# Conditional residual layer: two copies of W1 go to GpSimd, more seeds, more W1 by id, and a key for every step

## The chip, the core and the metric

The kernel runs on one core of one Trainium2 chip. The core has five engines that each work through their own list of instructions in order: TensorE (PE in the profile, with its weight loads as PEld), VectorE (DVE), ScalarE (ACT), GpSimd (POOL) and SyncE (SP), which here issues nearly all DMAs. They wait for each other through semaphores. The metric is the device time of one launch in microseconds; smaller is better.

## The reference

There are 128 batches. Each has x of 128 rows and 512 columns (float32), and an id between 0 and 8 that picks one of ten sets of weights.

```python
w1 = W1[id]; w2 = W2[id]                       # 512x128, 128x512
h = relu(x @ w1 + b1[id])
y = x + h @ w2 + b2[id]
mean, var = moments of y over the 512 columns
out = x + (y - mean) * rsqrt(var + 1e-5) * gamma[id] + beta[id]
```

All of it is float32. x and out are 33.5 MB each.

## The kernel before

All ten sets of weights end up on chip as tables: W1 (`w1`), W2 (`w2`), and b2, gamma and beta spread over the 128 partitions (`b2_b`, `gamma_b`, `beta_b`). A batch then goes through these steps, in a software pipeline of several batches; the line numbers are those of the profile.

- SyncE loads x for four batches at a time, 1 MB, into one of four buffers (`load_x`, L83).
- TensorE turns x into x transposed, four matmuls against the identity (`transpose_x`, L330), and ScalarE copies it out of PSUM (`copy_xT`, L334).
- W1 of the batch's id is brought into a small tile `w1s`, of which there are seven buffers. In most batches ScalarE copies it from the table (`stage_w1`, L321). The first 17 batches load it from memory by id (L173).
- TensorE multiplies, "down" (L353, four matmuls into the one tile `ph`), ScalarE adds b1 and takes the relu (`relu`, L361), TensorE multiplies again, "up" (L375, or L367 in a seeded batch), into one of five tiles `ys` in PSUM.
- y = x + up + b2 needs one addition of x and one of b2. In a batch of kind P, GpSimd adds x and b2 into a tile r ahead of time (`add_b2`, L340; four buffers), and VectorE adds r to the result and sums its columns in one pass (`residual`, L393). In a batch of kind E, the "seeded" ones, ScalarE copies x into the PSUM tile before the up, which then adds onto it (`seed`, L316), and the residual adds the row of `b2_b`. A few early batches have b2 added by VectorE (L385), the first two and the last two by a matmul.
- ScalarE squares and sums (`square`, L416), takes the mean (L407) and the root (L426); VectorE refines the root in three short steps (L430, L432, L435), scales by gamma (`scale`, L459) and adds onto x + beta (`finish`, L468). GpSimd has put x + beta into the output tile before (`add_beta`, L347).
- SyncE stores a pair of batches, 512 KB, from one of eight pair tiles `os` (`store`, L472).

Letters for the turn of a batch: in an "F" batch, two in 16, x comes in by DMA a second time in blocks (L290) and VectorE finishes the transpose (`turn_blocks`, L302), so that TensorE has no transposes and ScalarE no copy; its W1 comes by id in matching rows (L296). In a "w" batch, one in 16, W1 is loaded by id (`load_late`, L582). All others are "T".

The order in which each engine gets its steps is a plan. Every step has a key, which is a batch number plus an offset; all steps are sorted by key and issued in that order, and each engine's own list is kept in it (`keep`). Offsets stand in small tables, one for the middle (`BATCH`, `PAIR`) and one for the edges (`BATCH_EDGE`, `EDGE`), so that every batch of a region has the same offsets:

```python
BATCH = dict(turn=0.19, copy=0.16, r=-0.36, beta=-0.13, relu=1.26, w1=-0.77, up=2.66, load=-5.59, r_late=0.22)
SEED = {'E': 1.69}
```

A store's key is just behind the key of its pair's second finish. The work ahead of batch 4 and the last eight or so batches (from E = 123 on, and parts of the five before) are written out by hand, outside the plan.

Of the kernel before, what the change touches and what calls it, by code (L numbers as in the profile page):

```python
# [13 lines left out]
ET = mybir.EngineType  # L14
# [3 lines left out]
G = 4  # L18
# [1 line left out]
FIRST = 17  # L20
EARLY = 17
LATE = 17
U = 2
MIDDLE = 26
TURNED = 32
LAST = 4
KINDS = 'EPPPPPEPEPPPEPPP'
TURNS = 'TTTTFTTTTwTTFTTT'
SEEDED = 'E'
ON_GPSIMD = 'P'  # L30
BATCH = dict(turn=0.19, copy=0.16, r=-0.36, beta=-0.13, relu=1.26, w1=-0.77, up=2.66, load=-5.59, r_late=0.22)
BATCH_EDGE = dict(copy=0.2, r=0.05, r_late=1.05, beta=1.06, relu=1.3, w1=-0.6, up=2.5)
SEED = {'E': 1.69}
PAIR = dict(stat=0.22, square=0.34, means=1.98, root=1.9, scale0=3.03, n1=2.43, n2=3.115, n3=3.28, scale1=3.4, end0=3.67, end1=4.32)
EDGE = dict(stat=0.6, square=0.68, means=1.75, root=1.77, scale0=2.64, n1=2.65, n2=3.592, n3=3.62, scale1=3.64, end0=3.66, end1=4.66)


@with_exitstack
def cond_resid_kernel(ctx: ExitStack, tc: tile.TileContext, x, itok, W1, b1, W2, b2, gamma, beta, out):
# [39 lines left out]
    E = B - 5  # L79
# [6 lines left out]
    def xb(b):  # L86
        return xs[b // G][:, b % G, :]
# [5 lines left out]
    w1 = const.tile([P, L, KC, A], FP, name="w1")  # L93
# [34 lines left out]
    parts = const.tile([P, H], BF, name="parts")  # L128
# [14 lines left out]
    lids, w1s = {}, {}  # L143
# [8 lines left out]
    def lid(b, engine):  # L152
        g = b // G
        if (g, engine) not in lids:
            loads, vals = nc.values_load_multi_w_load_instructions(
                lang[0:1, g * G : (g + 1) * G],
                engines=[engine],
                min_val=0,
                max_val=L - 1,
                skip_runtime_bounds_check_because="clamped on the chip to 0..L-1 above",  # L160
            )
            for ins in loads:
                keep(ins)
            lids[g, engine] = vals
        return lids[g, engine][b % G]
# [95 lines left out]
    xT, hT, rs, os, ys, ssqs, nmeans, rstds = {}, {}, {}, {}, {}, {}, {}, {}  # L261
    phs, pxs, sums = {}, {}, {}


    def b2_by_matmul(b):
        return b in (0, 1) or b >= B - 2

    def kind(b):
        return KINDS[b % len(KINDS)] if MIDDLE <= b < B - LAST else "-"

    def turn(b):
        return TURNS[b % len(TURNS)] if TURNED <= b < B - LAST - 2 else "-"

    def seeded(b):
        return kind(b) in SEEDED

    def b2_on_gpsimd(b):
        return kind(b) in ON_GPSIMD or kind(b) == "-" and not b2_by_matmul(b) and not b2_by_vector(b)

    def b2_by_vector(b):  # L280
        return kind(b) == "-" and (b in (2, 3, 9, 13, 17, 21) or 24 <= b < B - 8 and (b % 16 in (1, 6, 11) or b % 32 == 30))

    x2s = {}

# [32 lines left out]

    def stage_w1(b):
        w1s[b] = wp.tile([P, KC, A], FP, tag="w1s", name=f"w1s_{b}")
        src = w1.rearrange("p l k a -> p (l k a)")[:, bass.ds(lid(b, ET.Activation) * (KC * A), KC * A)]  # L320
        keep(nc.scalar.copy(w1s[b].rearrange("p k a -> p (k a)"), src))  # L321

    def transpose_x(b):
        pxs[b] = p_x.tile([P, KC, P], FP, tag="xT", name=f"pxT_{b}")
# [11 lines left out]
    def add_b2(b):  # L336
        if b2_on_gpsimd(b):
            rs[b] = rp.tile([P, H], FP, tag="r", name=f"r_{b}")
            v = lid(b, ET.Pool)
            keep(nc.gpsimd.tensor_tensor(rs[b], xb(b), b2_b[:, bass.ds(v * H, H)], ALU.add))  # L340

    def add_beta(b):
        g, j = divmod(b, 2)
        if j == 0:
            os[g] = op.tile([P, 2, H], FP, tag="o", name=f"o_{g}")
        v = lid(b, ET.Pool)
        keep(nc.gpsimd.tensor_tensor(os[g][:, j, :], xb(b), beta_b[:, bass.ds(v * H, H)], ALU.add))  # L347
# [61 lines left out]
    def square(b):  # L409

        g, j = divmod(b, 2)
        if j == 0:
# [61 lines left out]
    def on(b):  # L474
        return 0 <= b < B
# [172 lines left out]
    def at(when, step, *args):  # L648
        plan.append((when, len(plan), step, args))

    for b in range(B):
        when = BATCH_EDGE if kind(b) == "-" else BATCH
        if b >= 20 and b % G == 0:
            at((11 if b == 20 else b - 7) - 0.01, load_x, b // G)
        if b >= 3:
            for n, engine in ((b + 5, ET.Activation), (b + 5, ET.PE), (b + 6, ET.Pool)):
                if on(n):
                    at(b + 0.99, lid, n, engine)
        if turn(b) in "Fw":
            at(b + BATCH["load"] - 1, lid, b, ET.SP)  # L660
            at(b + BATCH["load"], load_rows if turn(b) == "F" else load_late, b)
        if turn(b) == "F":
            at(b + BATCH["load"], load_blocks, b)
            at(b + BATCH["turn"], turn_blocks, b)
        elif 5 <= b <= E - 2:
            at(b, transpose_x, b)
            at(b + when["copy"], copy_xT, b)
        if 4 <= b <= E - 3:
            at(b + (when["r"] if seeded(b) else when["r_late"]), add_b2, b)
            at(b + when["beta"], add_beta, b)  # L670
            at(b + 1.1, down, b)
            at(b + when["relu"], relu, b)
        if seeded(b):
            at(b + SEED[kind(b)], seed, b)
        if FIRST <= b <= E - 1 and turn(b) not in "Fw":
            at(b + when["w1"], stage_w1, b)
        if 2 <= b <= E - 4:
            at(b + when["up"], up, b)
# [4 lines left out]
    def at_pair(g, when, step, *args):  # L683
        if g < E // 2 - 3 or (step, *args) in begun:
            at(2 * g + 3 + when, step, *args)

    for g in range(E // 2 - 1):
        b = 2 * g
        when = EDGE if "-" in (kind(b), kind(b + 2)) else PAIR
        for j in (0, 1):  # L690
            at_pair(g, j + when["stat"] - 0.01, vector_b2, b + j)
            at_pair(g, j + when["stat"], residual, b + j)
            at_pair(g, j + when["square"], square, b + j)
        at_pair(g, when["means"], scalar_means, g)
        at_pair(g, when["root"], deviation, g)
        if b % G == 0 and on(b + G):
            at_pair(g, when["end0"] + 0.001, lid, b + G, ET.DVE)
        for n in (1, 2, 3):
            at_pair(g, when[f"n{n}"], rstd, g, n)
        for j in (0, 1):  # L700
            at_pair(g, when[f"scale{j}"], scale, b + j)
            at_pair(g, when[f"end{j}"], finish, b + j)
# [14 lines left out]
    copy_xT(E - 1)  # L717
    residual(E - 4)
    square(E - 4)
    rstd(E // 2 - 3, 3)  # L720
    relu(E - 2)
# [5 lines left out]
    end_of(E - 7)  # L727
    residual(E - 3)
    stage_w1(E)
    beta_of(E - 1)  # L730
    scalar_means(E // 2 - 2)
# [164 lines left out]
```

## Time and profile before

| what | value |
|---|---|
| median of three runs | 301.42 us (300.80 and 1073.14 the others) |
| profiled execution | 301.23 us, span 298.8 us |
| granted TensorE clock | 0.997 |
| busy: PE, DVE | 97%, 97% |
| busy: ACT, POOL | 93%, 93% |
| DMA | 85.48 MB, mean 286 GB/s, queue of SP 85.1% of 16 engines |

The span runs from the first to the last instruction; the profiled execution's own time has 2.4 us around it. Times of parts are read from the span. Busy shares are averages over the start (tables are loaded and spread, up to some 20 us), the long middle and the end (some 20 us), so the middle is looked at by itself. "L353" is line 353 of the kernel before.

### The profile page before, as it was taken

How to read it: one execution, taken by the hardware profiler on the slowest of the kernel's cores; microseconds unless marked ns; L12 is line 12 of the kernel's file. 1: busy time of each engine (PE TensorE's matmuls, PEld its weight loads, DVE VectorE, ACT ScalarE, POOL GpSimd, SP SyncE). 2: the span in 40 equal slices, each digit the busy share in tenths (PEclk: the TensorE clock that was granted, in tenths of full speed). 3: DMA queues.
4: the chain of work that ended last, by engine and by line, in shares of the span. 5: the costliest groups of instructions: out<-in, count | busy, mean ns of one | idle time of the engine just before them, and what ended most of it. 6: DMA issues, size and time to landing. Idle time of an engine off the chain costs nothing.

```text
span 298.8 us, 7251 instructions
## 1 busy us (share of the span) xinstructions
PE 290.7 (97%) x1783; PEld 214.7 (72%) x1783; DVE 288.9 (97%) x775; ACT 277.2 (93%) x766; POOL 277.4 (93%) x233
## 2 busy tenths in 40 slices
PE   7899999999999999999999999999999999999993
PEld 3758777777777777777777777777777777777761
DVE  6989999999999999999999999999999999999995
ACT  5868789999999999999999999999999999999983
POOL 1299998999999999999999999999999999999962
PEclk9999999999999999999999999999999999999998
DMA  6999999996799697988888887898988698894715
GB/s 233 369 393 370 342 329 396 400 325 212 270 297 328 169 378 218 321 316 284 277 280 295 275 283 256 281 300 224 356 256 269 233 313 301 250 349 163 237 73 219
DMA packets 61195, 85.48 MB, mean 286 GB/s; under 512 B 3641, under 2 KB 25156, under 8 KB 61154
## 3 DMA queue, kind: packets, MB, share of 16 engines
q1 hardware_dynamic: 61094, 84.97, 85.1%
q8 instruction: 15, 0.25, 0.3%
q14 instruction: 26, 0.21, 0.2%
q10 hardware_dynamic: 60, 0.05, 0.1%
HBM read 51.45 MB, written 33.55 MB: 284 GB/s over the span
## 4 chain that ended last, share of the span: by engine, by line
PE 81%; DVE 6%; ACT 4%; DMA 3%; issue 3%; SPq 1%; DVEq 0%; POOL 0%; ACTq 0%; POOLq 0%
PE ph L353 33%; PE py L375 26%; PE pxT L330 15%; PE py L367 7%; DMA w<-in_L_cond_W_dram 3%; DVE py L393 2%; ACT sq L416 1%; DVE o L553 1%; DVE py L459 1%; ACT w1s L321 1%; ACT xT L334 1%; SPq L173 1%; DVE n L559 0%; ACT hT L361 0%; ACT root L426 0%
## 5 line engine op out<-in xcount | busy, mean ns | idle before, releaser
L347 POOL TENSOR_TENSOR o<-x,beta_b 128x512 f32<-128x512 f32 x121 | 155.8, 1306 | 12.9 <-DVE beta_b L259 11.6
L353 PE MATMUL ph<-xT,w1s 128*128 128x128 f32 x1024 | 136.4, 276 | 0.1
L353 PEld LDWEIGHTS ph<-xT,w1s 128*128 128x128 f32 x1024 | 125.0, 192 | 8.7 <-ACT hT L361 7.0
L340 POOL TENSOR_TENSOR r<-x,b_b 128x512 f32<-128x512 f32 x89 | 116.1, 1305 | 0.0
L375 PE MATMUL py<-w,hT 128*128 x208 | 106.7, 595 | 0.7 <-DMA w<-in_L_cond_W_dram 0.7
L330 PEld LDWEIGHTS pxT<-ident,x 128*128 128x128 f32 x468 | 60.4, 150 | 60.6 <-issue 41.6
L459 DVE SCALAR_TENSOR_TENSOR py<-py,nmean,gamma_b 128x512 f32<-128x512 f32 x124 | 93.3, 753 | 0.0
L468 DVE SCALAR_TENSOR_TENSOR o<-py,rstd,o 128x512 f32<-128x512 f32 x116 | 86.8, 748 | 0.0
L416 ACT ACTIVATE sq<-py,sum 128x512 f32<-128x512 f32 x124 | 85.6, 690 | 0.7 <-DVE rstd L435 0.2
L334 ACT COPY xT<-pxT 128x512 f32<-128x512 f32 x117 | 67.8, 580 | 6.0 <-PE pxT L330 5.8
L330 PE MATMUL pxT<-ident,x 128*128 128x128 f32 x468 | 71.2, 275 | 0.9 <-ACT gamma_b L244 0.7
L393 DVE SCALAR_TENSOR_TENSOR py<-py,r 128x512 f32<-128x512 f32 x94 | 64.9, 690 | 1.4
L321 ACT COPY w1s<-w 128x512 f32 x91 | 56.7, 623 | 0.0
L361 ACT ACTIVATE hT<-ph,b1T 128x128 f32<-128x128 f32 x128 | 47.6, 372 | 5.1 <-PE ph L353 3.4
L375 PEld LDWEIGHTS py<-w,hT 128*128 128x128 f32 x208 | 31.7, 192 | 2.1 <-DMA w<-in_L_cond_W_dram 1.2
L416 ACT ACTIVATION_READ_ACCUMULATOR sq<-py,sum 128x1 f32 x124 | 25.9, 209 | 0.0
L367 PE MATMUL py<-w,hT 128*128 x48 | 25.3, 610 | 0.0
L393 DVE SCALAR_TENSOR_TENSOR py<-py,b_b 128x512 f32<-128x512 f32 x24 | 16.6, 693 | 1.5 <-PE py L367 1.4
L426 ACT ACTIVATE root<-ssq,eps 128x2 f32<-128x2 f32 x62 | 16.5, 266 | 1.5
L316 ACT COPY py<-x 128x512 f32<-128x512 f32 x24 | 14.4, 599 | 0.0
L393 DVE DVE_READ_ACCUMULATOR py<-py,r 128x1 f32 x94 | 13.2, 140 | 0.0
L407 ACT ACTIVATE nmean<-sum 128x2 f32<-128x2 f32 x61 | 11.7, 192 | 0.0
(79 smaller groups left out, 139.8 us busy)
## 6 DMA issues: line engine op xcount, KB each, us to landing
out_dram<-o SPq DMA_DIRECT2D x62, 512.0 KB, 4.0
x<-in_x_dram SPq DMA_DIRECT2D x27, 1024.0 KB, 7.7
w1s<-in_L_cond_W_dram SPq DMA_DIRECT2D x26, 256.0 KB, 7.3
x<-in_x_dram SPq DMA_DIRECT2D x10, 512.0 KB, 6.0
w1s<-in_L_cond_W_dram SPq DMA_DIRECT2D x44, 64.0 KB, 3.2
x<-in_x_dram SPq DMA_DIRECT2D x44, 64.0 KB, 2.1
w<-in_L_cond_W_dram SPq DMA_DIRECT2D x4, 640.0 KB, 8.1
w<-in_L_cond_W_dram SPq DMA_DIRECT2D x1, 1792.0 KB, 10.2
```

The lines of the kernel that those rows point to most:

```text
L321: keep(nc.scalar.copy(w1s[b].rearrange("p k a -> p (k a)"), src))
L330: keep(nc.tensor.transpose(pxs[b][:, k, :], cols, ident))
L334: keep(nc.scalar.copy(xT[b], pxs.pop(b)))
L340: keep(nc.gpsimd.tensor_tensor(rs[b], xb(b), b2_b[:, bass.ds(v * H, H)], ALU.add))
L347: keep(nc.gpsimd.tensor_tensor(os[g][:, j, :], xb(b), beta_b[:, bass.ds(v * H, H)], ALU.add))
L353: nc.tensor.matmul(phs[b], lhsT=w1s[b][:, k, :], rhs=xT_of(b, k), start=(k == 0), stop=(k == KC - 1))
L361: keep(nc.scalar.activation(hT[b], phs.pop(b), AF.Relu, bias=b1T[:, bass.ds(lid(b, ET.Activation), 1)]))
L375: keep(nc.tensor.matmul(ys[b], lhsT=hT[b], rhs=w2[:, bass.ds(v * H, H)], start=not m, stop=True))
L393: nc.vector.scalar_tensor_tensor(ys[b], ys[b], 1.0, r, ALU.mult, ALU.add, accum_out=sum_of(b))
L416: nc.scalar.activation(sq, ys[b], AF.Square, bias=col(sums, b), scale=-float(H), accum_out=col(ssqs, b))
L459: nc.vector.scalar_tensor_tensor(ys[b], ys[b], col(nmeans, b), gamma_b[:, bass.ds(v * H, H)], ALU.add, ALU.mult)
L468: nc.vector.scalar_tensor_tensor(o, ys[b], rstds[g][:, j : j + 1], o, ALU.mult, ALU.add)
```

## The change

Kinds and turns are now given in three strings: for the first 32 batches, for 16 that repeat from batch 32 to 111, and for the last 16.

- In the repeating part, seeded batches go from 4 in 16 (positions 0, 6, 8, 12) to 6 (0, 2, 6, 10, 12, 14). The other batches there have b2 added by GpSimd, as before. In the last 16 batches one is seeded (three before).
- "w" (W1 loaded by id) is at positions 0, 1, 2 (before: 9); in the last 16 at six batches (before one). "F" stays at 4 and 12, and at batch 116.
- A new turn, "c": `stage_w1` of such a batch is a `tensor_copy` on GpSimd in place of the copy on ScalarE, from the same table. Positions 8 and 14, and batch 121.
- Every step of every batch has its own offset, from a table `STEPS`: 32 values, then 16 that repeat, then 16. The loads of x have theirs in `X_STEPS`. Stores have keys of their own, too.
- An output tile or a tile of square sums is taken by whichever batch of the pair comes first.

```diff
-KINDS = 'EPPPPPEPEPPPEPPP'
-TURNS = 'TTTTFTTTTwTTFTTT'
+KINDS = ('MMDDPPPPPDPPPDPPPDPPPDPPPPPPEPPP', 'EPEPPPEPPPEPEPEP', 'PPEPPPPPPPPPPPMM')
+TURNS = ('TTTTTTTTTTTTTTTTTTTTTTTTTTTTTTTT', 'wwwTFTTTcTTTFTcT', 'TwTwFwwwwcTTTTTT')
...
+STEPS = {
+    "load": (
...
+        (-2.78, -1.96, -3.28, 0, -4.24, 0, 0, 0, 0, 0, 0, 0, -6.24, 0, 0, 0,),
...
+    "w1": (
...
+        (0, 0, 0, -0.79, 0, -0.39, 0.09, 0.85, -6.2, -3.35, -0.9, 0.28, 0, -0.7, -0.27, 0.84,),
...
+    "r": (
...
+        (0, -0.77, 0, -0.57, -0.65, -1.15, 0, 0.4, -0.76, 2.76, 0, -0.94, 0, 1.5, 0, -0.07,),
...
+    "beta": (
...
+        (3.06, 2.96, 3.37, 0.46, 1.58, 1.99, 6.71, 0.2, 3.13, 4.31, 3.02, 0.91, 1.54, 3.21, 3.09, 1.68,),
...
+    "seed": (
...
+        (2.02, 0, 1.67, 0, 0, 0, 2.48, 0, 0, 0, 2.47, 0, 2.61, 0, 1.99, 0,),
...
+    "up": (
...
+        (2.17, 2.66, 2.8, 2.96, 2.74, 3.14, 3.06, 2.78, 1.91, 2.39, 3.48, 3.29, 2.74, 2.34, 2.55, 2.25,),
...
+    "stat": (
...
+        (3.3, 3.55, 3.48, 3.28, 3.91, 3.8, 3.42, 3.71, 3.93, 4.05, 3.71, 3.51, 3.38, 2.83, 2.98, 2.77,),
...
+    "store": (
...
+        (10.03, 0, 11.56, 0, 16.12, 0, 11.81, 0, 9.84, 0, 15.6, 0, 15.03, 0, 17.49, 0,),
...
+X_STEPS = (-3.47, -3.9, -4.25, -6.5, -4.71, -2.89, -2.66, -6.5, -4.71, -2.89, -2.66, -6.5, -4.71, -2.89, -2.66, -6.5, -4.71, -2.89, -2.66, -6.5, -4.71, -2.89, -2.66, -4.38, -3.47, -7.32, -6.03)
...
     def stage_w1(b):
         w1s[b] = wp.tile([P, KC, A], FP, tag="w1s", name=f"w1s_{b}")
-        src = w1.rearrange("p l k a -> p (l k a)")[:, bass.ds(lid(b, ET.Activation) * (KC * A), KC * A)]
-        keep(nc.scalar.copy(w1s[b].rearrange("p k a -> p (k a)"), src))
+        gpsimd = turn(b) == "c"
+        v = lid(b, ET.Pool if gpsimd else ET.Activation)
+        src = w1.rearrange("p l k a -> p (l k a)")[:, bass.ds(v * (KC * A), KC * A)]
+        dst = w1s[b].rearrange("p k a -> p (k a)")
+        keep(nc.gpsimd.tensor_copy(dst, src) if gpsimd else nc.scalar.copy(dst, src))
...
+    def when(name, b):
+        return b + of(STEPS[name], b)
+
     for b in range(B):
-        when = BATCH_EDGE if kind(b) == "-" else BATCH
         if b >= 20 and b % G == 0:
-            at((11 if b == 20 else b - 7) - 0.01, load_x, b // G)
+            at(b + X_STEPS[b // G - 5], load_x, b // G)
...
-            at(b + 1.1, down, b)
-            at(b + when["relu"], relu, b)
+            at(when("down", b), down, b)
+            at(when("relu", b), relu, b)
...
-        at_pair(g, when["end1"] + 0.001, store, g)
+        at_pair(g, when("store", b), store, g)
```

"stat" is the key of a residual, "r" of `add_b2`, "load" of the loads of an F or w batch; `of` picks the value of a batch from the three parts. The other steps (transposes, copies, downs, relus, squares, means, roots, scales, finishes) have rows of the same form. Nothing in the hand-written start and end is edited.

More of the change, by code (lines that the diff above doesn't have):

```diff
@@ L277, in b2_on_gpsimd @@
     def b2_on_gpsimd(b):
[L278 removed]
+        return kind(b) in ON_GPSIMD
     def b2_by_vector(b):
[L281 removed]
+        return kind(b) == "D"
     x2s = {}
@@ L681, in cond_resid_kernel, with at_pair @@
     begun += [(scalar_means, E // 2 - 3), (deviation, E // 2 - 3), (scale, E - 7), (rstd, E // 2 - 3, 1)]
-    def at_pair(g, when, step, *args):
+    def at_pair(g, key, step, *args):
         if g < E // 2 - 3 or (step, *args) in begun:
-            at(2 * g + 3 + when, step, *args)
+            at(key, step, *args)
     for g in range(E // 2 - 1):
         b = 2 * g
[L689 to L695, printed above, removed]
-        if b % G == 0 and on(b + G):
[L697 to L702, printed above, removed]
-        at_pair(g, when["end1"] + 0.001, store, g)
+        for n in (b, b + 1):
+            if b2_by_vector(n):
+                at_pair(g, when("vb2", n), vector_b2, n)
+            at_pair(g, when("stat", n), residual, n)
+            at_pair(g, when("square", n), square, n)
+        at_pair(g, when("means", b), scalar_means, g)
+        at_pair(g, when("root", b), deviation, g)
+        for n in (1, 2, 3):
+            at_pair(g, when(f"n{n}", b), rstd, g, n)
+        for n in (b, b + 1):
+            at_pair(g, when("scale", n), scale, n)
+            at_pair(g, when("end", n), finish, n)
+        if b % G == 0 and on(b + G):
+            at_pair(g, when("scale", b) + 0.001, lid, b + G, ET.DVE)
+        at_pair(g, when("store", b), store, g)
```

85 lines of the change are left out of this document (58 added, 27 removed), and 62 rows, old and new, of the table STEPS.

## The prediction

> **What bounds the kernel now.** I read the page's busy times first, then the stretches of the middle, the chain that ended last, and the waits, in that order, because the busy shares alone do not choose between four engines.
>
> ```profile
> span 298.8 us, 7251 instructions
> ...
> PE 290.7 (97%) x1783; PEld 214.7 (72%) x1783; DVE 288.9 (97%) x775; ACT 277.2 (93%) x766; POOL 277.4 (93%) x233
> ```
>
> ```profile
> 120.00:154.60 34.60, 34.60 (x217) 25.79 (x216) 34.03 (x91) 33.88 (x96) 34.60 (x29) 1.00 0.88 290
> 154.60:189.20 34.60, 34.60 (x219) 25.87 (x218) 34.23 (x91) 34.05 (x96) 34.60 (x29) 1.00 0.86 282
> 16.50:291.00 274.50, 274.50 (x1704) 205.20 (x1705) 270.09 (x715) 261.94 (x733) 270.79 (x221) 1.00 0.86 286
> ```
>
> The columns of a stretch are its length, then the busy time of PE, weight loads, DVE, ACT and POOL, the granted clock, the DMA share and GB/s. In the two middle stretches PE and POOL are busy all the time, DVE and ACT for 34.0 to 34.2 of 34.6 us. The third row says more: from 16.5 to 291.0 us PE is never idle, at clock 1.00. So the question is only how much of PE's time is longer than its work needs.
>
> ```profile
> 154.95 1.02 PE py L367 x2
> ...
> 156.41 0.89 PE ph L353 x8
> 157.30 0.86 PE py L375 x2
> 158.16 0.97 PE ph L353 x8
> ...
> 160.43 0.89 PE ph L353 x8
> 161.32 0.86 PE py L375 x2
> 162.18 0.44 PE pxT L330 x4
> 162.62 0.89 PE ph L353 x8
> ...
> 184.10 1.05 PE ph L353 x8
> ...
> 189.54 1.02 PE py L367 x2
> ```
>
> These are pieces of the chain (start, length, what). A plain batch is 0.89 (down) + 0.86 (up) + 0.44 (transposes) = 2.19 us, the distance from 160.43 to 162.62. A batch turned by DMA and VectorE ("F", two in 16) has no transposes: 1.75 us. Sixteen batches need 14 x 2.19 + 2 x 1.75 = 34.16 us. The two seeded ups at 154.95 and 189.54 lie 16 batches apart: 34.59 us. So PE loses **0.43 us in 16 batches**, in visible places: 0.16 at a seeded up (1.02 for 0.86), 0.08 at each down after an F batch's (0.97 for 0.89), 0.16 at 184.10 (1.05 for 0.89).
>
> ```profile
> PEld ph L353 <- ACT hT L361: 7.0, 13, 0.6
> ...
> POOL o L347 <- DMA out_dram<-o: 1.3, 1, 1.3
> ```
>
> From the list of waits (total us, times, longest): where a down waits, it is for ScalarE's relu ahead of it. POOL waits for a store's buffer once in the whole run. Everything below is measured against these 34.16 and 34.59 us. The table for single steps covers batches 32 to 122, so 91/16 = 5.7 such periods.
>
> **The change part by part.** Prices:
>
> ```profile
> L347 POOL TENSOR_TENSOR o<-x,beta_b 128x512 f32<-128x512 f32 x121 | 155.8, 1306 | 12.9 <-DVE beta_b L259 11.6 <-DMA out_dram<-o 1.3
> ...
> L321 ACT COPY w1s<-w 128x512 f32 x91 | 56.7, 623 | 0.0
> ...
> L316 ACT COPY py<-x 128x512 f32<-128x512 f32 x24 | 14.4, 599 | 0.0
> ...
> masks.py:197 POOL MEMSET ident<- 128x128 f32 x1 | 0.2, 204 | 0.0
> ...
> L882 POOL MEMSET const-float32-0.0<- 128x1 f32 x1 | 0.1, 98 | 0.3 <-issue 0.3
> ```
>
> ```profile
> 153.65 1.30 POOL L340 TENSOR_TENSOR r<-x,b_b 128x512 f32<-128x512 f32 x1
> ...
> 154.89 1.30 POOL L347 TENSOR_TENSOR o<-x,beta_b 128x512 f32<-128x512 f32 x1
> ...
> 156.12 1.30 POOL L340 TENSOR_TENSOR r<-x,b_b 128x512 f32<-128x512 f32 x1
> ```
>
> - **ScalarE.** Of 16 batches, W1 was copied by ScalarE in 13, and is in 9 (two go to GpSimd, two more are loaded by id); the seeds go from 4 to 6. Per period: -4 x 0.623 + 2 x 0.599 = -1.29 us of 33.9 to 34.1. Over the kernel, counted in the plan: 26 copies fewer and 8 seeds more, -11.4 us. In the last 16 batches alone, W1 copies fall from 8 to 2 (batches 112 to 120) and seeds from 3 to 1.
> - **GpSimd.** A seeded batch needs no addition of b2 there: -2 additions per period, +2 copies of W1. Additions start 1.23 us apart (153.65, 154.89, 156.12), so 28 of them were 34.5 us. No copy on POOL is in the trace. From below: a memset writes 512 columns in 98 + 511 x (204 - 98)/127 = 525 ns; from above, an addition with two inputs, 1231 ns. A copy reads one operand, between none and two, so I take the middle, 0.88 us: 26 x 1.231 + 2 x 0.88 = 33.8 us (33.1 and 34.5 at the ends). Nothing is lost at either end. [...]
> - **VectorE, TensorE.** Counts unchanged: 16 residuals, scales and finishes, 24 short steps, 2 turns; 14 transposes, 16 downs, 16 ups. A seeded batch's residual reads b2's row where the others read r. So the 34.16 us of PE stay as the floor, and the first 16.5 us (until W2 has landed) and the last 8, written out by hand, hold the same instructions.
> - **DMA.** W1 by id goes from 1 to 3 in 16: two more loads of 256 KB per period, 15 more in all, 3.9 MB beside 85.5.
>
> ```profile
> 28.00:44.00 16.00, 16.00 (x102) 12.59 (x102) 15.76 (x41) 12.67 (x38) 16.00 (x14) 1.00 1.12 332
> 48.00:60.00 12.00, 12.00 (x76) 8.84 (x75) 12.00 (x34) 11.73 (x32) 12.00 (x11) 1.00 1.05 397
> ...
> w<-in_L_cond_W_dram SPq DMA_DIRECT2D x4, 640.0 KB, 8.1
> ```
>
>   In 48 to 60 us the queue has only x and stores and is full: 397 GB/s. In 28 to 44 us about half the 5.3 MB are the four parts of the W1 table (2.6 MB, in 512 B pieces as the loads by id): 332 GB/s, so those pieces move at about 285 GB/s (1/332 = 0.5/397 + 0.5/285). A period then needs 8.39 MB/0.397 + 7 x 0.262/0.285 = 27.6 us of 34.6, 25.7 before. On average the queue holds.
> - **The order.** Each step now has its own key, so every engine's sequence changes; durations don't. What changes is how long before its use a thing is ready, and in what order SP issues. Stores were keyed just behind their last finish; now 9 to 17 batches behind their pair, so SP no longer sits waiting for VectorE, but issues loads and stores in bursts.
>
> *Sum.* ScalarE gets 1.29 us of air per period, and the visible PE losses are waits for ScalarE (relu, seed). I take half of the 0.43 us as gone, since two more seeds are two more such places: 0.21 x 5.7 = 1.2 us. The profiled execution is 301.23 us (298.8 of span, 2.4 around it), 0.2 below the median of 301.42. 301.2 - 1.2 = **300.0 us**. If all 0.43 goes, 298.8; with 1 us more, allowed for the untouched tail that starts behind a freer ScalarE, 297.8. That is the low end: no mechanism here takes PE below 34.16.
>
> **Rivals.**
>
> *A store stuck behind loads (slower).* In the steady table W1 of batch 64 is loaded into the buffer that down(60) frees; until then SP stands. Then it issues, in this order: W1 of 64, store of pair 25, W1 of 66 and of 65, x of 68 to 71, store of pair 23. Pair 31's o tile (batches 62, 63) reuses pair 23's, so GpSimd's add_beta(63) waits for that last store.
>
> ```profile
> DMA to landing us min/median/max: 3.5/3.9/4.0
> ```
>
> ```profile
> 151.54 0.70 DVE L393 SCALAR_TENSOR_TENSOR py<-py,r 128x512 f32<-128x512 f32 x1
> ...
> 152.16 0.75 DVE L468 SCALAR_TENSOR_TENSOR o<-py,rstd,o 128x512 f32<-128x512 f32 x1
> ...
> 152.82 0.15 DVE L430 SCALAR_TENSOR_TENSOR part<-ssq,root 128x2 f32<-128x2 f32 x1
> ...
> 152.89 0.75 DVE L459 SCALAR_TENSOR_TENSOR py<-py,nmean,gamma_b 128x512 f32<-128x512 f32 x1
> ...
> 153.55 0.15 DVE L432 SCALAR_TENSOR_TENSOR part<-part,root 128x2 f32<-128x2 f32 x1
> ```
>
> A lone store (first row: 512 KB from issue to landing in the middle of the run) takes at best 3.5 us, 1.3 of it transfer at 397 GB/s, so 2.2 us are fixed. The stuck store lands 0.4 + 0.786/0.285 + 2.097/0.397 + 2.2 = 10.6 us after SP is let go. From there GpSimd works 14 additions and a copy up to r of batch 71, which sits near its residual in the table (14 x 1.231 + 0.88 = 18.1); VectorE then has 3 residuals, 2 finishes, 2 scales, 3 short steps and the turn of batch 76 (steps of 0.62, 0.66, 0.66 and 0.07 from the rows, and 0.7: 5.4), and down(76) frees the next load. With down(60)'s own 0.9 and a release of 0.1 the ring is **35.1 us**: 0.5 above 34.59. It closes three times (stores of pairs 23, 31, 39): +1.5 us. It decides from a landing of 10.1 us on. With the whole 2.88 MB at the 282 GB/s of the period's mean it is 12.8 us and the ring 37.3: +8.1 us. Times 302.7 to 309.4, middle 304. For it: GpSimd has no idle time to catch up with, and the key of that store stands 1.2 batches ahead of the addition that needs its buffer, 8.5 before. Against it: the queue is empty when the burst starts, and GpSimd's sum per period falls by 0.7 us. [...]
>
> *Seeds too late (slower).* Before, every seed stood 0.97 of a batch ahead of its up in the order; now two of six (positions 0 and 12) stand 0.15 and 0.13 ahead, 0.3 us for a copy of 0.6. Each would cost from the 0.16 us seen at 154.95 to its full 0.60: 0.3 to 1.2 per period, five periods with this table, +1.6 to +6.0: 302.8 to 307.2. Against it: keys order a queue and are no times; ScalarE, lighter now, may reach the seed early.
>
> *Relief that nobody needs (no effect).* DVE is busy 34.2 of 34.6 too; if VectorE's chain sets the pace, ScalarE's air buys nothing: 301.2.
>
> *All losses gone:* 297.8 to 298.8.
>
> **How the numbers follow.** Half the losses gone, 299.2 to 300.8: 0.40. No effect, 300.8 to 301.8: 0.17. Stuck store: 0.25, a third of it above 307.3. Late seeds: 0.11, a quarter above that. All losses gone: 0.05. Something unseen in the new order: 0.02, above. About 2% is what a measurement of this kernel tells from no change: below 295.4 or above 307.4. Faster by that much would need more than PE's floor allows: 0.02, for a mistake in the floor. Slower: 0.08 + 0.03 + 0.02, rounded to 0.14. The range goes from 297.8 to 307.0: it leaves out the slow ends of both rivals and a little below the floor.
>
> **What would show it.** In the chain of the changed kernel, two seeded ups 16 batches apart should lie 34.3 to 34.5 us apart; 35 or more between 130 and 240 us speaks for the stuck store, above all if POOL shows waits for out_dram<-o of several us and DVE waits for r. Seeded ups of 1.0 to 1.4 us speak for late seeds. ACT's busy sum should be near 266 us, POOL's copies between 0.5 and 1.2 us each. I am wrong if ScalarE is idle by 1 us more per period and PE's period is still 34.59, or if PE shows idle time in the first 32 batches, whose order I took as harmless.

## The result, and the profile after

The changed kernel takes **311.19 us** (median of four runs, 309.20 to 314.18) beside 301.13 us for the kernel before on the same chip: a ratio of 1.0316, 95% interval 1.0219 to 1.0412. It is slower. Ratios, here and below, are of fast runs alone: this one leaves out the run of 314.18 us and, of the kernel before, one of 1073.14 us. The forecast was 300.0 us with a range up to 307.0; both are wrong. The profiled execution took 309.2 us, 307.4 of them span; it is the fastest of the four.

The page of the changed kernel, its span and busy times:

```profile
span 307.4 us, 7270 instructions
...
PE 294.8 (96%) x1783; PEld 218.2 (71%) x1783; DVE 290.4 (94%) x775; ACT 268.8 (87%) x748; POOL 273.7 (89%) x236
```

ScalarE has the 26 copies fewer and 8 seeds more that were counted, but is 8.4 us less busy (277.2 us before), where 11.4 was forecast. DVE and POOL are within 4 us of before. Of PE's 4.1 us more, 1.7 lie in the first 22 us, where they delay nothing (f3 below has them too and is no slower), and 1.7 come from a slower clock in the tail, below. The time is in gaps. Its stretches (length; busy PE, weight loads, DVE, ACT, POOL; granted clock, DMA share, GB/s):

```profile
120.00:154.60 34.60, 33.15 (x209) 24.77 (x208) 32.40 (x87) 31.56 (x90) 28.59 (x25) 1.00 0.95 304
154.60:189.20 34.60, 34.60 (x220) 26.23 (x219) 34.39 (x91) 33.26 (x94) 34.60 (x30) 1.00 0.91 298
255.00:275.00 20.00, 17.65 (x104) 13.56 (x103) 16.59 (x43) 14.18 (x41) 14.23 (x12) 0.91 0.93 285
```

The second stretch looks as before: PE never idle. In the first, PE lacks 1.45 us and GpSimd stands for 6.0; in the third PE lacks 2.35 us and the granted clock is 0.91. Before, PE was busy and the clock was 1.00 in all three; the third was:

```profile
255.00:275.00 20.00, 20.00 (x128) 15.04 (x127) 19.64 (x53) 19.75 (x58) 20.00 (x17) 1.00 0.75 255
```

To place the loss, I compare the start of each batch's relu in the two traces. The patterns of 16 differ, so lags are compared at the same position of the 16 (32, 48, 64 and so on):

```
batch            32     48     64     80     96    112    114    116    121    124    end
after - before +0.11  +0.24  +1.76  +1.55  +1.36  +1.30  +1.40  +5.53  +6.42  +6.39  +8.62
```

So there is a step of 1.5 us between batches 48 and 64 (at batch 61: +0.11 at 60, +1.89 at 61), then a gain of 0.2 us in each 16 batches up to 96, then a loss of 7.3 us from batch 112 to the end. From the list of waits (total, times, longest), the first row has grown (7.0, 13, 0.6 before), the others are new or longer:

```profile
PEld ph L468 <- ACT hT L476: 16.3, 35, 2.2
...
POOL o L462 <- DMA out_dram<-o: 8.0, 3, 6.0
...
POOL r L455 <- DVE py L508: 3.9, 1, 3.9
...
PE ph L468 <- DMA w1s<-in_L_cond_W_dram: 2.3, 1, 2.3
...
POOL r L455 <- DMA x<-in_x_dram: 1.9, 1, 1.9
```

**The step at batch 61.** The trace in order of time (start, length, engine and line; in brackets the idle time before, and what ended it):

```profile
130.34 0.93 SPq L187 DMA_DIRECT2D x<-in_x_dram  x2
131.32 2.12 SPq L587 DMA_DIRECT2D out_dram<-o  x3
...
142.20 4.94 POOL L462 TENSOR_TENSOR o<-x,beta_b 128x512 f32<-128x512 f32 x4 [5.96 <-DMA out_dram<-o]
...
144.73 0.75 DVE L583 SCALAR_TENSOR_TENSOR o<-py,rstd,o 128x512 f32<-128x512 f32 x1 [2.13 <-POOL o L462]
...
145.53 0.70 PE L490 MATMUL py<-w,hT 128*128 x1 [1.29 <-DVE o L583]
```

SP issues x for batches 60 to 63 and for 64 to 67, 1 MB each, and behind them the store of pair 21, issued at 131.32 and landed at 142.13: 10.8 us, where a store of the kernel before took 3.5 to 4.0 between 120 and 160 us. GpSimd's add_beta of batch 59 needs that pair's output tile and stands 5.96 us, with beta of 54 queued behind it; VectorE's finish waits for that beta, and an up waits for VectorE.

**The tail.** The same view, SP's loads and what waits for them:

```profile
247.19 1.47 SPq L187 DMA_DIRECT2D x<-in_x_dram  x2
248.91 1.94 SPq L408 DMA_DIRECT2D w1s<-in_L_cond_W_dram  x4
...
250.95 8.58 SPq L402 DMA_DIRECT2D x<-in_x_dram  x4
...
259.33 1.28 POOL L455 TENSOR_TENSOR r<-x,b_b 128x512 f32<-128x512 f32 x1 [1.90 <-DMA x<-in_x_dram]
...
260.79 2.74 SPq L697 DMA_DIRECT2D w1s<-in_L_cond_W_dram  x3
...
265.88 1.96 PE L468 MATMUL ph<-xT,w1s 128*128 128x128 f32 x8 [2.35 <-DMA w1s<-in_L_cond_W_dram]
...
273.09 1.27 POOL L455 TENSOR_TENSOR r<-x,b_b 128x512 f32<-128x512 f32 x1 [3.88 <-DVE py L508]
...
294.44 1.16 PE L468 MATMUL ph<-xT,w1s 128*128 128x128 f32 x8 [1.95 <-ACT hT L476]
```

Before, SP issued the same four blocks in 2 us:

```profile
252.02 2.04 SPq L290 DMA_DIRECT2D x<-in_x_dram  x4
```

Now the four blocks for batch 116 take SP 8.58 us to issue. In this trace SP's 242 DMAs use eight semaphores in turn, and in the 88 cases in which it tells the landing of the DMA eight places ahead, none starts before that landing. So the third block goes out at 255.11, when x of 116 to 119 (issued at 247.19) has landed at 255.09, and the fourth at 259.21, when x of 120 to 123 (issued at 248.29) has landed at 259.20. W1 of batch 115 stands behind them: issued at 260.79, landed at 265.74. Down(115) waits for it. Two windows tell what the stop costs:

```profile
266.00:269.40 3.40, 3.40 (x14) 2.88 (x15) 1.89 (x3) 0.98 (x4) 3.21 (x3) 0.50 1.06 384
...
258.00:265.80 7.80, 5.53 (x33) 3.65 (x31) 7.06 (x21) 5.77 (x16) 6.47 (x6) 1.00 0.77 233
```

Right behind the stop the granted clock is 0.50 for 3.41 us: 2.35 of waiting and half of 3.41 make 4.06 us, and the relus go from +1.40 to +5.53. The DMA engines are busy only 0.77 of the stretch ahead of the stop: SP stood, not the queue.

The last 2.2 us (+6.39 at batch 124, +8.62 at the end) are lost in the hand-written end. GpSimd had stood 3.88 us up to 273.09 for VectorE to free a buffer of r. The chain that ended last goes through GpSimd's additions for the last batches, up to 292.15, and PE stands 1.95 us up to 294.44.

### The profile page after: what moved, and what is told of

It is laid out like the page before. It is cut to its first block, busy times and chain, and to the rows that moved or that the text cites. A ratio compares the mean times of both kernels' runs of the same rounds, so it can differ in the third digit from the quotient of the medians.

```text
span 307.4 us, 7270 instructions
## 1 busy us (share of the span) xinstructions
PE 294.8 (96%) x1783; PEld 218.2 (71%) x1783; DVE 290.4 (94%) x775; ACT 268.8 (87%) x748; POOL 273.7 (89%) x236
## 5 line engine op out<-in xcount | busy, mean ns | idle before, releaser
L462 POOL TENSOR_TENSOR o<-x,beta_b 128x512 f32<-128x512 f32 x121 | 151.5, 1279 | 20.7 <-DVE beta_b L363 12.7
L468 PEld LDWEIGHTS ph<-xT,w1s 128*128 128x128 f32 x1024 | 127.9, 193 | 27.5 <-ACT hT L476 16.3
L455 POOL TENSOR_TENSOR r<-x,b_b 128x512 f32<-128x512 f32 x81 | 102.3, 1279 | 5.9 <-DVE py L508 3.9
L583 DVE SCALAR_TENSOR_TENSOR o<-py,rstd,o 128x512 f32<-128x512 f32 x116 | 84.2, 746 | 3.7 <-POOL o L462 2.4
L508 DVE SCALAR_TENSOR_TENSOR py<-py,r 128x512 f32<-128x512 f32 x86 | 59.5, 692 | 3.1 <-POOL r L607 2.1
L436 ACT COPY w1s<-w 128x512 f32 x65 | 40.1, 618 | 0.9 <-issue 0.9
L490 PEld LDWEIGHTS py<-w,hT 128*128 128x128 f32 x192 | 29.3, 192 | 3.7 <-DVE o L583 1.9
L508 DVE SCALAR_TENSOR_TENSOR py<-py,b_b 128x512 f32<-128x512 f32 x32 | 22.0, 689 | 0.0
L428 ACT COPY py<-x 128x512 f32<-128x512 f32 x32 | 19.0, 592 | 0.0
L508 DVE DVE_READ_ACCUMULATOR py<-py,r 128x1 f32 x86 | 12.1, 140 | 0.0
```

Of the source, the lines that this page charges most:

```text
L436: keep(nc.gpsimd.tensor_copy(dst, src) if gpsimd else nc.scalar.copy(dst, src))
L468: nc.tensor.matmul(phs[b], lhsT=w1s[b][:, k, :], rhs=xT_of(b, k), start=(k == 0), stop=(k == KC - 1))
L490: keep(nc.tensor.matmul(ys[b], lhsT=hT[b], rhs=w2[:, bass.ds(v * H, H)], start=not m, stop=True))
L508: nc.vector.scalar_tensor_tensor(ys[b], ys[b], 1.0, r, ALU.mult, ALU.add, accum_out=sum_of(b))
L583: nc.vector.scalar_tensor_tensor(o, ys[b], rstds[g][:, j : j + 1], o, ALU.mult, ALU.add)
```

## The experiments

The tables have three parts: the first 32 batches, the 16 that repeat from 32 to 111, and the last 16. Lags below are starts of relus against the kernel before, from the profiled executions. Here they are for most of the runs:

```
batch                              48     64     96    112    114    116    118    121    end
after                           +0.24  +1.76  +1.36  +1.30  +1.40  +5.53  +5.50  +6.42  +8.62
e1 tail as before               +0.30  +1.69  +3.70  +4.55  +4.47  +4.39  +4.74  +4.74  +4.62
e2 only the tail changed        -0.14  -0.33  -0.33  -0.88  +1.03  +8.33 +14.06 +16.18 +16.36
e3 W1 of 115 copied             +0.32  +5.05  +4.46  +4.28  +4.57  +4.31  +7.79  +9.17  +9.27
e4 stores at once               +6.35  +8.23 +13.09 +14.75 +14.85 +23.76 +27.67 +29.21 +29.27
f1 store ahead, tail as before  +1.30  +0.89  +0.71  +3.87  +3.80  +3.71  +4.06  +4.07  +4.22
f3 work of the middle alone     -0.70  -1.04  -1.35  -0.66  -0.66  -0.66  -0.66  -0.66  -0.80
g1 store and x ahead            +0.61  +0.18  -0.07  -0.02  +0.08  +4.80  +4.77  +5.69  +7.86
g3 copies without more seeds    +0.10  +0.92  +2.95  +3.94  +3.95  +3.99  +3.94  +3.95  +3.97
g4 one late W1                  -0.30  -0.47  -0.43  -0.42  -0.63  +6.49  +6.63  +6.63  +6.57
h1 work of the tail alone       -0.17  -0.33  -0.31  -0.25  -0.67  -0.65  -0.68  +0.78  +1.56
h2 all work, no new order       -0.97  -1.30  -1.61  -1.13  -1.55  -1.53  -1.56  -1.57  -1.18
h3 tail, DMAs as before         +0.95  +0.76  +0.76  +0.20  +2.11 +12.36 +12.89 +13.81 +17.73
f6 tail, r of 120 later         -0.06  -0.23  -0.21  -0.75  +1.17  +7.93 +14.36 +15.82 +16.00
i1 h3 and r of 120 later        -0.35  -0.53  -0.54  -1.09  +0.83  +1.62  +6.73  +8.76 +12.66
i2 three mends                  +0.20  -0.09  +0.52  +0.28  +0.45  +0.34  +7.71 +10.11 +11.96
```

### Which part of the table

Two rivals at first: the tail loses all but a little, or the store at batch 60 starts everything. The first kernel (e1) has the last 16 batches as before, kinds, turns and offsets; the second (e2) has only them changed.

```diff
-KINDS = (..., 'PPEPPPPPPPPPPPMM')
-TURNS = (..., 'TwTwFwwwwcTTTTTT')
+KINDS = (..., 'EPPPPPEPEPPPPPMM')
+TURNS = (..., 'TTTTFTTTTwTTTTTT')
```

> The last 16 batches (112 to 127) have the kinds, the turns and all keys of the kernel before; the first 32 and the repeating 16 stay changed. Tail theory (the loss is made in the last 16 batches, because W1 of batch 115 lands late and GpSimd falls behind there): the 7 us between batch 113 and the end go, what stays is +1.8 us at batch 60 and three to five periods that gain 0.2 us each: 301 to 303 us. Store theory of the prediction (the loss is made in the repeating part, by stores behind loads): 307 us or more, because that part is kept.

> The opposite: the first 32 and the repeating 16 as before, the last 16 as changed. Tail theory: 306 to 310 us. Store theory: 300 to 303 us.

Measured: e1 306.01 us, 1.0196 [1.0155, 1.0237]; e2 316.66 us, 1.0536 [1.0517, 1.0554]. Neither lies in a range that one of the two named: both parts lose by themselves. In e1 nothing is lost behind batch 112 (+4.55 to +4.62), and GpSimd's wait at batch 59 comes back at 91 and 107. The row of e1's list of waits that grew:

```profile
POOL o L462 <- DMA out_dram<-o: 10.8, 4, 4.8
```

In e2 the loss is all behind 112, and more than twice that of the changed kernel, in two stops of PE for W1 (of 115 and 118). Rows of e2's list of waits:

```profile
PE ph L468 <- DMA w1s<-in_L_cond_W_dram: 9.4, 2, 4.8
POOL r L455 <- DMA x<-in_x_dram: 7.3, 1, 7.3
```

### Work or order

The next kernel (f3) has the middle's kinds and turns (six seeds, three loads by id, two copies on GpSimd), but every step at the offset that the kernel before gives it, in all three parts.

```diff
-KINDS = (..., 'EPPPPPEPEPPPEPPP', ...)
-TURNS = (..., 'TTTTFTTTTwTTFTTT', ...)
+KINDS = (..., 'EPEPPPEPPPEPEPEP', ...)
+TURNS = (..., 'wwwTFTTTcTTTFTcT', ...)
```

> The kernel before with only the work of the repeating 16 changed: 6 seeds, 3 loads of W1 by id, 2 copies of W1 on GpSimd; all offsets stay the uniform ones of before, in all three parts. If the order is what costs and the work is harmless, PE's period falls to 34.2 to 34.5 us and the run is 299 to 301 us. If the added loads or the seeds cost by themselves, 303 us or more.

Measured: **299.79 us** (299.72 to 299.87), 0.9960 [0.9946, 0.9974]. The work alone is 1.2 us faster than the kernel before (0.8 to 1.6 by the interval). From batch 48 to 96 its lag falls from -0.70 to -1.35. Its page, a stretch, and two seeded ups of its chain, 16 batches apart:

```profile
PE 291.7 (98%) x1783; PEld 216.8 (73%) x1783; DVE 288.4 (97%) x775; ACT 273.8 (92%) x756; POOL 270.6 (91%) x233
...
154.60:189.20 34.60, 34.60 (x218) 26.10 (x217) 34.32 (x92) 33.51 (x95) 34.60 (x31) 1.00 0.91 296
...
158.33 0.99 PE py L482 x2
...
192.76 0.99 PE py L482 x2
```

They lie 34.43 us apart, 34.59 before: PE gains 0.16 us in 16 batches. The lag at 112 is back at -0.66, since the old pattern starts there, and at the end it is -0.80: five periods of 0.16.

A smaller piece (g3): only the two copies on GpSimd, with the four seeds and one load by id of before.

```diff
-TURNS = (..., 'TTTTFTTTTwTTFTTT', ...)
+TURNS = (..., 'TTTTFTTTcwTTFTcT', ...)
```

> The kernel before with only the two copies of W1 on GpSimd in 16 batches (positions 8 and 14), 4 seeds and 1 load by id as before, offsets of before. ScalarE gives up 1.25 us per period, GpSimd takes 2 copies of 0.61 us on top of its 28 additions of 1.23 us: 35.7 us in a period of 34.6. If GpSimd's sum then sets the pace: 305 to 308 us. If GpSimd had more air than its busy row shows: 300 to 301 us.

Measured: 305.07 us, 1.0141 [1.0124, 1.0158]. It loses about 1.0 us per 16 batches from batch 48 on. Downs wait for the copy (from its list of waits), and the copy itself is short (from its groups: busy sum, mean ns):

```profile
PE ph L468 <- POOL w1s L436: 3.8, 4, 1.0
```

```profile
L436 POOL COPY w1s<-w 128x512 f32 x10 | 6.1, 609 | 0.0
```

28 additions of 1.231 us and two copies of 0.57 (their distance in the changed kernel's trace) are 35.6 us, 1.0 more than the period of 34.58. So GpSimd sets the pace there; the two further seeds, which take two additions off it, are what pays for the copies.

### The store behind the loads

f1 is e1 with one value changed: the store of position 10 goes ahead of the two x loads.

```diff
-        (10.03, 0, 11.56, 0, 16.12, 0, 11.81, 0, 9.84, 0, 15.6, 0, 15.03, 0, 17.49, 0,),
+        (10.03, 0, 11.56, 0, 16.12, 0, 11.81, 0, 9.84, 0, 15.3, 0, 15.03, 0, 17.49, 0,),
```

> The changed first 32 and repeating 16 batches, the last 16 as before, and one number more: the store key of position 10 goes from 15.6 to 15.3, so that SyncE issues the store of pair 21 (29, 37, 45) ahead of two loads of x of 1 MB each instead of behind them. Stuck store: GpSimd no longer waits 4 to 6 us for that store at batches 59 and 91, the jumps of PE there (1.3 and 1.9 us in the run with only the old tail) go: 301.5 to 303.5 us. If the jumps come from the bursts of DMA as such, the loads of x are late instead, or another store: 305 to 306.5 us.

Measured: 302.83 us, 1.0057 [1.0031, 1.0084], 3.2 us less than e1 (4.2 by the two ratios). The profiled execution is the slowest of its six (304.8 us): its lag is +0.7 up to batch 96 and +3.9 at 112, so something in this order still slips at times; in this trace PE waits 1.33 us for x at 238.00. In two other kernels with this one value changed (g1, i2), the middle ends at -0.02 and +0.28.

The opposite test (e4): in the changed kernel, every store goes right behind its last finish, as before. The row of the repeating part (the other two are changed in the same way):

```diff
-        (10.03, 0, 11.56, 0, 16.12, 0, 11.81, 0, 9.84, 0, 15.6, 0, 15.03, 0, 17.49, 0,),
+        (7.851, 0, 7.481, 0, 7.451, 0, 8.071, 0, 7.211, 0, 7.221, 0, 6.871, 0, 7.191, 0,),
```

> The changed kernel with every store of the plan keyed right behind the last finish of its pair, as before; all other keys stay. Store theory: the wait of 6.0 us of GpSimd for a store at batch 59 goes, and with it 1.8 us and any other such ring: 305 to 307.5 us or less. Tail theory: the 1.8 us go at the most, and may come back because SyncE then waits for VectorE ahead of its loads: 307 to 310 us.

Measured: 331.17 us, 1.1011 [1.0991, 1.1031]; both theories missed. Rows of its list of waits:

```profile
POOL r L455 <- DMA x<-in_x_dram: 20.2, 5, 7.4
PE ph L468 <- DMA w1s<-in_L_cond_W_dram: 8.9, 2, 6.1
DVE xT L414 <- DMA x<-in_x_dram: 7.5, 3, 3.4
```

What SP itself waits for, from the waits of its queue:

```profile
SPq L587 <- DVE part L547: 52.4, 15, 8.7
SPq L587 <- DVE o L583: 51.8, 17, 10.1
```

SP stands with a store in hand for VectorE, 104 us in these two rows, and the loads stand behind. The table loads x 2.7 to 7.3 batches ahead where the kernel before has 7.0, so, as I read it, it bears no store that waits. The stores' places and the loads' places go together.

### The tail, place by place

If W1 of 115 is the place, taking it off the queue should help. In e3, ScalarE copies it from the table, in the changed kernel. In g2, x of 116 to 119 gets the offset of before, so that it doesn't hold the blocks; g1 is g2 with the store at 15.3.

```diff
-TURNS = (..., 'TwTwFwwwwcTTTTTT')
+TURNS = (..., 'TwTTFwwwwcTTTTTT')
...
-X_STEPS = (..., -4.38, -3.47, -7.32, -6.03)
+X_STEPS = (..., -4.38, -7.01, -7.32, -6.03)
```

> The changed kernel, but W1 of batch 115 is copied from the table by ScalarE instead of loaded by id; nothing else is edited. If the late W1 and the slower TensorE clock that follows its wait start the tail's loss: TensorE does not stop at batch 115, the clock stays at 1.00 there, 304 to 306.5 us against the 309.2 of the profiled changed kernel. If GpSimd's delay (its waits of 1.9 and 3.9 us at about 257 and 269 us) is the cause by itself, the end comes hardly sooner: 308 to 310 us, and VectorE waits for GpSimd instead.

> The changed kernel with one number: the load of x of batches 116 to 119 is keyed 7.01 ahead of batch 116, as before, instead of 3.47, so it no longer goes out 1.1 us ahead of the next load of x and right in front of the F loads of 116 and W1 of 115. If W1 of 115 is late because SyncE has eight DMAs in flight and must wait for those two loads to land: it is issued some 5 us sooner, TensorE does not stop there, the clock stays at 1.00, and the run is 304 to 307 us. If the queue of DMA is too full there in any order, something else is late: 308 us or more.

> Both one-number edits on the changed kernel: the store of position 10 at 15.3, and x of 116 at -7.01. If the two delays add up: 1.5 to 3 us under the run with x of 116 alone, 302 to 305 us. If SyncE's order has more such places, 306 us or more.

Measured: e3 310.73 us, 1.0339 [1.0308, 1.0370]; g2 313.39, 1.0394 [1.0373, 1.0415]; g1 310.77, 1.0337 [1.0311, 1.0364]. In e3 the loss at 115 is gone (+4.57 to +4.31 from 114 to 116), and part of it comes at 118 and 121: from batch 112 to the end e3 loses 5.0 us, the changed kernel 7.3. The median hardly moves, and in the trace the step at batch 61 is 4.7 us instead of 1.5, with the same kernel there: PE stands 3.14 us. So the size of one such step differs from one execution to the next. In g2 x of 116 still goes out at 247.43, since SP is held by earlier transfers, and W1 of 115 lands later still, at 269.24. In g1 the middle is flat and the tail loses 7.9 us all the same. Moving one transfer mostly moves the stop.

In the tail alone (e2), f5 loads W1 of 115 and 117 1.5 batches earlier; f6 puts GpSimd's addition of b2 for batch 120 later, f7 does both.

```diff
-        (0, -2.98, 0, -1.14, -2.84, -3.13, 0.69, -4.14, 2.02, 0, 0, 0, 0, 0, 0, 0,),
+        (0, -2.98, 0, -2.6, -2.84, -4.58, 0.69, -4.14, 2.02, 0, 0, 0, 0, 0, 0, 0,),
...
-        (2.3, 0.35, 0, 3.01, 1.97, 1.96, 1.16, 8.66, -6.35, 0, 0, 0, 0, 0, 0, 0,),
+        (2.3, 0.35, 0, 3.01, 1.97, 1.96, 1.16, 8.66, -0.1, 0, 0, 0, 0, 0, 0, 0,),
```

> The first 112 batches as before, the last 16 as changed (316.7 us), and two numbers: W1 of 115 and of 117 are issued ahead of the loads of x of batches 116 to 123, instead of behind these and the loads of F batch 116. If the late W1 starts the loss of the last 16: 304 to 309 us. If GpSimd's addition for batch 120, which waits for that x at the head of its queue, is the cause by itself: 313 to 317 us.

> The same base as the run with W1 earlier (316.7 us), with one number: GpSimd's addition of x and b2 for batch 120 stands at 119.9 instead of 113.65, behind those of 112 to 118. If that addition holds GpSimd up (7.3 us of wait for x in the base): 307 to 311 us. If the late W1 is the cause: 313 to 317 us.

> The kernel before with the table of the last 16 batches, W1 of 115 and 117 loaded 1.5 batches earlier, and b2's addition for batch 120 at -0.1. Alone these gave 320.1 and 316.3. If each of them fell to the other's fault: 302 to 308. If W1 of 118 behind the stores, or x behind the loads, takes their place: 312 or more.

Measured: f5 320.13 us, 1.0637 [1.0618, 1.0655]; f6 316.31, 1.0504 [1.0483, 1.0524]; f7 315.43, 1.0481 [1.0464, 1.0499], where e2 had 316.66. None of them mends it: f7, the best, is 1.2 us below e2 (1.7 by the ratios), and f5 lies above both ranges that were named for it. In f5 GpSimd's wait for x grows to 11.0 us (7.3 in e2), since W1 now goes ahead of x.

### Work or order, in the tail

h1 has the tail's work (one seed, six loads by id, one copy on GpSimd) at the offsets of before. h2 has the whole of the change's work, all three parts, at these offsets. h3 is e2 with only the DMAs' offsets as before: W1 by id 5.59 ahead, x 7.01 ahead, stores behind their finish. The edit of h3, with the rows of "load" and "store":

```diff
-        (0, -2.98, 0, -1.14, -2.84, -3.13, 0.69, -4.14, 2.02, 0, 0, 0, 0, 0, 0, 0,),
+        (0, -5.59, 0, -5.59, -5.59, -5.59, -5.59, -5.59, -5.59, 0, 0, 0, 0, 0, 0, 0,),
...
-        (14.28, 0, 13.17, 0, 0, 0, 0, 0, 0, 0, 0, 0, 0, 0, 0, 0,),
+        (9.271, 0, 12.171, 0, 1.001, 0, 1.001, 0, 1.001, 0, 1.001, 0, 1.001, 0, 1.001, 0,),
...
-X_STEPS = (..., -4.38, -3.47, -7.32, -6.03)
+X_STEPS = (..., -7.01, -7.01, -7.01, -7.01)
```

> The kernel before, with the last 16 batches' kinds and turns of the change (one seed, six W1 by id, one W1 copied by GpSimd), but every step of them at the offsets of before (W1 by id 5.59 batches ahead, x 7.01 ahead). Theory 1, the order of the table loses the 16 us of the tail alone: 300 to 302.5, no wait of TensorE for W1 above 1 us. Theory 2, six loads by id in nine batches are too much for a queue with few transfers under way, in whatever order: 306 or more, with waits of TensorE for W1 of several us near 115 to 120.

> The kinds and turns of the change in all three parts, every step at the offsets of before. If work costs nothing and all losses are the table's order: 299.0 to 300.5, the steady part 1 us ahead as with the repeating part alone (299.79). If the tail's work loses by itself: as much above 299.8 as the run of the tail's work alone is above the kernel before.

> The kernel before with the whole table of the last 16 batches, except the keys of the DMAs SyncE issues: loads by id 5.59 ahead, x 7.01 ahead, stores just behind their last finish. The tail alone took 316.7. If the place of the loads in SyncE's list is what loses: 300 to 304. If the order of the engines' own steps loses (GpSimd held up by an addition of b2 for batch 120 that is put too early, or the like): 308 or more.

Measured: h1 302.23 us, 1.0058 [1.0041, 1.0075]; h2 300.12, 0.9985 [0.9967, 1.0003]; h3 317.15, 1.0540 [1.0518, 1.0561]. h1 and h3 have the same work, and the same loads at the same offsets: in both, x of 120 to 123 lands late, at 267.3 and 267.9 us (262.7 before). What differs is the order of the engines' steps, with the stores, which follow their finishes in both; it is worth 14.9 us. GpSimd in h3, in order of time:

```profile
253.41 2.56 POOL L455 TENSOR_TENSOR r<-x,b_b 128x512 f32<-128x512 f32 x2
268.06 1.26 POOL L455 TENSOR_TENSOR r<-x,b_b 128x512 f32<-128x512 f32 x1 [12.09 <-DMA x<-in_x_dram]
269.28 1.26 POOL L462 TENSOR_TENSOR o<-x,beta_b 128x512 f32<-128x512 f32 x1
270.50 1.26 POOL L455 TENSOR_TENSOR r<-x,b_b 128x512 f32<-128x512 f32 x1
```

The table puts r of batch 120 (key 113.65) ahead of beta and r of batch 112 (114.02, 114.30). GpSimd stands 12.09 us for x of batch 120, with work for 112 behind it, and VectorE and PE follow. In h1, GpSimd at 267 us is still at work on earlier batches and never waits for x. h1's own 1.6 us come from the copy of W1 for batch 121, for which PE waits 1.5 us; in h2, where GpSimd has two additions fewer per period and is ahead, that wait is gone.

i1 is h3 with r of 120 at -0.1, and i2 is the changed kernel with that, with the DMAs of the tail as before, and with the store of position 10 at 15.3.

```diff
-        (2.3, 0.35, 0, 3.01, 1.97, 1.96, 1.16, 8.66, -6.35, 0, 0, 0, 0, 0, 0, 0,),
+        (2.3, 0.35, 0, 3.01, 1.97, 1.96, 1.16, 8.66, -0.1, 0, 0, 0, 0, 0, 0, 0,),
```

> The kernel before with the table of the last 16 batches, its DMAs at the offsets of before, and b2's addition for batch 120 at -0.1 in place of -6.35. If late loads and this one addition are the whole of the tail's loss: 300 to 304, GpSimd waits for x under 1 us. If other places of the engines' order lose too: 307 or more.

> The changed kernel with three mends: the store of position 10 at 15.3, the DMAs of the last 16 batches at the offsets of before, b2's addition for 120 at -0.1. If the three places are the whole loss: 299.5 to 302.5, first downs and relus as the kernel before up to batch 112 (as measured with the store's mend) and at most 2 us behind at the end. If a fourth place loses: 305 or more.

Measured: i1 311.43 us, 1.0336 [1.0299, 1.0373]; i2 311.63, 1.0298 [1.0259, 1.0336]. In i2 the middle is mended (+0.28 at 112, +0.34 at 116), the tail is not. GpSimd in i1, in order of time, and the stop of PE that follows:

```profile
257.03 1.29 POOL L455 TENSOR_TENSOR r<-x,b_b 128x512 f32<-128x512 f32 x1
268.10 2.49 POOL L462 TENSOR_TENSOR o<-x,beta_b 128x512 f32<-128x512 f32 x2 [9.78 <-DMA x<-in_x_dram]
...
274.38 1.01 PE L468 MATMUL ph<-xT,w1s 128*128 128x128 f32 x3 [4.54 <-ACT hT L476]
```

The wait is not gone but has moved one step on: add_beta of 120 (offset -2.09, key 117.91) stands ahead of beta of 114 and r of 115 to 118, and it needs the same x. f6 had shown it already, with 5.2 us. What both moved together would give was not tried.

### What one late W1 costs

The kernel before with one edit: W1 of 115 by id, and its load put so late that PE must wait.

```diff
-TURNS = (..., 'TTTTFTTTTwTTTTTT')
+TURNS = (..., 'TTTwFTTTTwTTTTTT')
...
-        (0, 0, 0, 0, -5.59, 0, 0, 0, 0, -5.59, 0, 0, 0, 0, 0, 0,),
+        (0, 0, 0, 0.4, -5.59, 0, 0, 0, 0, -5.59, 0, 0, 0, 0, 0, 0,),
```

> The kernel before, with W1 of batch 115 loaded by id on purpose too late, behind the store of batches 108 and 109. It measures what a stop of TensorE costs by itself. With a stop of 2.5 to 3.5 us: if the granted clock halves after it for 3.4 us, the run loses the stop and 1.5 to 2 us on top, 305 to 306.5 us; if the clock has nothing to do with it, only the stop, 303.5 to 304.5 us.

Measured: 307.91 us, 1.0242 [1.0221, 1.0263]. One down in order of time, and a stretch with its clock:

```profile
266.29 2.05 PE L468 MATMUL ph<-xT,w1s 128*128 128x128 f32 x8 [4.79 <-DMA w1s<-in_L_cond_W_dram]
...
263.80:270.50 6.70, 4.21 (x14) 3.10 (x15) 0.65 (x2) 1.43 (x5) 6.70 (x6) 0.50 0.78 235
```

The stop is 4.79 us. The clock is 0.50 over these 6.70 us, 4.21 of them with PE at work, where this down takes 2.05 us and the next one, at clock 1.00, 1.06. So I estimate that half of the 4.21 is lost: 4.79 + 2.1 = 6.9, and the lag goes from -0.63 to +6.49 (7.1). In a kernel whose PE has no slack this is final: it stays to the end (+6.57).

## Why the prediction was wrong, step by step

- **The bound, and the sum of 1.2 us: right in kind, somewhat large, and not what decided.** In f3 the period is 34.43 us, so 0.16 of PE's 0.43 us go (0.21 forecast), and over five periods 0.8 us, not 1.2. What is left are two seeded ups of 0.99 per period, as the prediction expected of more seeds. Before, only one of four seeded ups (1.02) and one of two downs behind an F batch (0.97) were long; "each" in the prediction's list is too much. That f3's median of 299.79 us comes so near 300.0 is partly luck: its trace gains 0.8 us. In the changed kernel too the middle gains 0.2 us per period from batch 64 to 96.
- **ScalarE: near.** 268.8 us busy (266 forecast). **GpSimd's copy: mis-sized, harmless.** I took 0.88 us between 0.525 and 1.231; the trace has

```profile
L436 ACT COPY w1s<-w 128x512 f32 x65 | 40.1, 618 | 0.9 <-issue 0.9
...
L436 POOL COPY w1s<-w 128x512 f32 x11 | 6.8, 615 | 0.0
```

  that is 0.615 us, as short as ScalarE's 0.618.
- **"On average the queue holds": true, and the wrong question.** The DMA share is 0.95 and 0.91 in the two stretches of the middle. What counted was when single transfers land: the 256 KB of W1 of 115 went out at 260.79, behind two blocks that had stood until two 1 MB loads had landed, at 255.09 and 259.20. An average over 16 batches hides it.
- **"Every engine's sequence changes; durations don't": this step failed.** I gave the new order no price but one ring and late seeds. All work in the old order costs nothing (h2: 0.9985); with the new order it is 1.0316. The order is the whole loss, some 10 us.
- **The stuck store (chance 0.25): mechanism right, place and size not.** It is pair 21's store (position 10), behind x of 60 to 67, not pair 23's, and GpSimd waits 5.96 us there as the rival described. It cost 1.5 us in the profiled run, 4.7 in e3's, and 3.2 to 4.2 us between e1 and f1. The 10.6 us of the ring assume that a queue moves what it holds one after another; no run shows that by itself, only that this store, issued behind 2 MB of x, landed after 10.8 us. My own list of SP's order followed one W1 through one period and did not look at the other stores.
- **The tail: the named failure.** I allowed up to 1 us of gain for "the untouched tail". Only its last batches are untouched; the last 16 have a row of the table of their own, with six loads by id in nine batches and GpSimd's r and beta of 120 put ahead of those of earlier batches. It cost 7.3 us. Nothing in the prediction read that row.
- **Late seeds (0.11): not seen.** PE's waits for a seed come to 0.2 us in all. **First 32 batches:** harmless, as taken: +0.11 us at batch 32, and PE is busy for 67.47 of the 67.50 us from 16.5 to 84.0.
- **What stays open:** which few values would mend the tail. Late W1, r and beta of 120 each show as a stop, and so does GpSimd's late arrival in the hand-written end, but no run mended all of them. In the middle only the store's place was tested by itself.

## What to carry to other kernels

When a change moves every step of an in-order schedule, price its order by itself: put the new work in the old order, and the difference is the schedule's. For each step that is moved forward, ask which load it needs and what stands behind it on its engine; a step put early costs nothing until its input is late, and then it holds back work that was ready. Read the first and last pieces of a table with the same care as the part that repeats, since there the loss can't be made good.

## What the runs showed of the hardware

With three long stops of PE the granted clock fell to 0.50. Behind the stop of 2.35 us in the changed kernel it was 0.50 for 3.41 us. With the stops of 4.79 us (g4, up to 266.29) and 4.81 us (e2, up to 268.01) it was 0.50 over whole stretches of 6.70 us, 263.80 to 270.50 and 266.00 to 272.70, that begin while PE still stands. In e1, whose longest wait of PE is 1.7 us, the mean granted clock of the profiled execution is 0.996, beside 0.997 in the kernel before. Two stops of 1.95 us came out differently; what followed them, first in i1, then in the changed kernel:

```profile
298.30:301.60 3.30, 3.30 (x12) 2.61 (x11) 2.74 (x10) 2.40 (x8) 2.36 (x2) 0.50 0.03 7
...
294.50:300.00 5.50, 5.50 (x26) 3.46 (x27) 5.36 (x20) 4.80 (x13) 4.68 (x5) 1.00 0.14 52
```

No run shows why these two differ. At 0.50 a down took 1.96 us (the changed kernel) and 2.05 us (g4), at 1.00 in g4 1.06. So by my estimate the stop of 2.35 us cost its length and 1.7 us on top, half of the 3.41, and that of 4.79 us its length and 2.1.

In the traces of the changed kernel and the kernel before, no DMA of SP starts before the one eight places ahead has landed, wherever they tell that landing (88 and 82 times), while some (22 and 12) start before the one seven places ahead has. With 1 MB loads among them, the four blocks of batch 116 took 8.58 us to issue (2.04 before). And GpSimd copied 128 x 512 floats in 0.57 us from start to start in the changed kernel, less than half the 1.23 us of its addition with two inputs.
